# Flamingo gated block on one core: the front reordered (filter, context loads, convolution 0, weights, norms)

## The chip, the cores and the metric

One Trainium2 core runs the whole program. The metric is device time in microseconds (us) of one execution, the median of the runs. The engines are named as in the profile: PE (TensorE matmuls) with PEld (its weight loads), DVE (VectorE), ACT (ScalarE), POOL (GpSimd) and SP (SyncE, here only an issuer of transfers). ACT and POOL issue transfers too. Each engine takes its instructions in order, so an instruction that waits holds up all that stands behind it on its engine.

## The reference, cut to what matters

```python
# x: (16, 256, 256) fp32, ctx: (16, 120, 256) fp32
z  = ctx @ W_in + b_in;  zn = layernorm(z) * g_ln + beta_ln
h  = silu(pe @ Wp1 + bp1) @ Wp2 + bp2            # implicit filter, 512 positions
w  = exp(-arange(512) * exp(a)) [:, None] * h
c  = causal_convolution(zn, w)                   # by FFT in the reference, along the sequence
y  = ffn1(layernorm(x)) * c[:, idx]              # ffn: layernorm, W1a, silu, W1b, + input
x  = x + tanh(g_xattn) * ffn2(y)                 # W2a, silu, W2b
# then a mixture of 16 experts, top 2 of each 32-wide head slice
t  = (layernorm(x) @ Wm + bm).reshape(-1, 32);   gates = top2(softmax(t @ expert_emb))
x  = x + tanh(g_ffn) * (combine(gates, gelu(t @ W1 + b1) @ W2 + b2) @ Wo + bo)
```

## The kernel before, in words

The 4,096 tokens are eight blocks of 512 (4 tiles of 128 tokens). Fp32 weights and activations are split in a high and a low part, and a product is three matmuls of those.

**The front** is ordered by the framework's scheduler from the program's order (up to L953, where `manual_schedule` begins); from there on the order is that of the code. First come the loads: SP's queue takes `cv`, the filter's inputs (`pe`, `Wp1`, `Wp2`), blocks 0 and 1 of x and the first MLP's weights (`w1a`, `w1b`); ACT's queue takes `W_in`, the context in four parts (`load_ctx`, tiles printed as `Y`, in whose storage they lie), `b_in`, `gz` and the rows `bc`. The filter: window exponential (L709), `pe @ Wp1` (L712), silu (L715), `@ Wp2` (L719), times the window (L724) to DRAM as `filt_d`, from which 16 Hankel tiles `hk` are loaded, three buffers deep. The context: eight groups of matmuls (L752 bias, L760), squares for the variance on ACT (L767), gain on DVE (L771); `context_root` (L778 and the steps of `rsqrt_some`, L146 to L165) gives `rz`. `context_norm` writes 32 slices of `zn`: for the first `by_pool` of them ACT scales (L788) and POOL adds the shift (L789), for the others DVE does both (L793).

**The first MLP** (`Mlp1`, blocks 0 to 7) has the steps norm (`normed`: with `off` on ACT, L184; without on DVE, L188), `turn` (transposes L235, copies L237 on ACT and L238 on DVE), `first` (matmuls L205, silu L259 and L260 on ACT, low part L268) and `second` (L293, L278), whose `done` adds the residual (L875) and multiplies by the convolution's result (L876, POOL).

**The convolution** has 16 steps: `conv_mm` (64 matmuls L899, copies `cvs` L906 on ACT, then the next `hk` load) and `conv_turn` (transposes L917, DVE). `mixed` interleaves it: for every second step of the first MLP it takes one step of `side` (the convolution), and for every step one of `weights` (`early_roots`, `early_weights`, which casts `w2` and `v2`). `Mlp2` (0 and 1), `Route(0)` and the first expert stacks are then ordered by hand: `mlp20` is `Mlp2(0)`, `mlp21` is `Mlp2(1)`. `behind_it` places `routes[1]`, `mlps[2]`, the lay-outs (`lay`, which send a normed block through DRAM) and `late_weights`, whose steps load and cast `wm`, `bd`, `wst` (L1035, L1036), and `Wo`.

**The main phase** starts at the first expert step, `hps` (L1257): 256 steps of matmul, gelu on ACT (L1262), second matmul (L1272), gate times output on DVE (L1280) and sum on POOL (L1282); the remaining blocks' MLPs and routes are spread among them.

Of the kernel before, what the change touches and what calls it, by code (L numbers as in the profile page):

```python
# [24 lines left out]
FP = mybir.dt.float32  # L25
FR = mybir.dt.float32r
I32 = mybir.dt.int32
AF = mybir.ActivationFunctionType
ALU = mybir.AluOpType
# [4 lines left out]
P = 128  # L34
# [11 lines left out]
NB = 8  # L46
# [18 lines left out]
XB = 5  # L65
# [28 lines left out]
def block_kernel(  # L94
# [3 lines left out]
    nc = tc.nc  # L98
    dram = ctx.enter_context(tc.tile_pool(name="dram", bufs=1, space=DRAM))
    base = ctx.enter_context(tc.tile_pool(name="base", bufs=1))  # L100
    const = ctx.enter_context(tc.tile_pool(name="const", bufs=1))
# [8 lines left out]
    Y = const.tile([P, NT, D], FP, name="Y")  # L110
    mv1 = const.tile([P, NT, 2], FP, name="mv1")
    mv2 = const.tile([P, NT, 2], FP, name="mv2")
    mv3 = const.tile([P, NT, 2], FP, name="mv3")
# [4 lines left out]
    def scalar(name, func):  # L118
        t = const.tile([P, 1], FP, name=f"s_{name}")
        nc.scalar.activation(t, col(name), func)  # L120
        return t
# [51 lines left out]
    def offset(mean, r, n):  # L173
        off = small.tile([P, n], FP, name="off", tag=f"off{n}", bufs=4 if n == 4 else 2)
        nc.vector.scalar_tensor_tensor(off, mean, -1.0, r, ALU.mult, ALU.mult)
        return off

    def normed(dst, src, mv, t0, r, off=None):

        mean = mv[:, t0 : t0 + 4, 0]  # L180
        for j in range(4):
            c = slice(j, j + 1)
            if off is not None:
                nc.scalar.activation(  # L184
                    dst[:, j, :], src[:, j, :], AF.Identity, bias=off[:, c], scale=r[:, c]
                )
            else:
                nc.vector.tensor_scalar(  # L188
                    dst[:, j, :], src[:, j, :], mean[:, c], r[:, c], ALU.subtract, ALU.mult
                )  # L190
# [126 lines left out]
    class Mlp2:  # L317
# [22 lines left out]
        def prep(self, pool=base, name="n"):  # L340
            t0 = 4 * self.i
            self.n = pool.tile([P, 4, D], FP, name=name, tag=name)
            normed(self.n, Y[:, t0 : t0 + 4, :], mv2, t0, self.r)

        def stream(self):
            t0 = 4 * self.i
# [42 lines left out]
    class Route:  # L389
# [9 lines left out]
        def prep(self):  # L399
            t0 = 4 * self.i  # L400
            y = Y[:, t0 : t0 + 4, :]
            self.n = base.tile([P, 4, D], FP, name="n", tag="n")
            normed(self.n, y, mv3, t0, self.r)

        def shift(self):
            y = Y[:, 4 * self.i : 4 * self.i + 4, :]
# [86 lines left out]
    def some(gen, n=1):  # L493
        for _ in range(n):
            next(gen, None)
# [42 lines left out]
    with ExitStack() as ph:  # L538
# [22 lines left out]
        xs, hankel = {}, {}  # L561

        bc = front.tile([P, NROW], FP, name="bc", bufs=1)
# [37 lines left out]
        window = f1[:, 3 * LF : 4 * LF]  # L601
# [10 lines left out]
        ctx_r = ctx_t.rearrange("(c p) n -> p c n", p=P)  # L612
# [5 lines left out]
        ]  # L618
        z_sb = free[:, NT * D // 2 :].rearrange("p (t j d) -> p t j d", j=4, d=P)

        def load_ctx(g):
            nc.scalar.dma_start(ctx_sb[g], ctx_r[:, :, bass.ts(g, 4 * P)])

        load_ctx(0)
        b_in = front.tile([P, D], FP, name="b_in")
# [10 lines left out]
            )  # L636
        load_x(0)
        for g in (1, 2, 3):
            load_ctx(g)
        w1a = staged(W1a.rearrange("(c p) n -> p c n", p=P), 2, DFF, nc.sync)  # L640
        nc.scalar.dma_start(bc, rows.partition_broadcast(P))
        w1b = staged(W1b.rearrange("(c p) n -> p c n", p=P), NM, D, nc.sync)
        load_x(1)

# [56 lines left out]
        nc.gpsimd.memset(filt, 0.0)  # L701


        ea = scalar("a", AF.Exp)
        tgx = scalar("g_xattn", AF.Tanh)
        tgf = scalar("g_ffn", AF.Tanh)
        nea = const.tile([P, 1], FP, name="nea")
        nc.vector.tensor_scalar(nea, ea, -1.0, None, ALU.mult)
        nc.scalar.activation(window, window, AF.Exp, scale=nea)  # L709
        for m, n in enumerate((P, P, DPOS)):  # L710
            ps = bank("second")
            nc.tensor.matmul(  # L712
# [65 lines left out]
            nc.tensor.matmul(out=var, lhsT=both, rhs=ss, start=True, stop=True)  # L778
            return rsqrt_eps("rz", var, 32, pool=front)

        def context_norm(rz, by_pool=12):
            for n in range(32):
                b, k = n // 2, n % 2
                dst = zn[:, :, k, b : b + 2 * B + 1 : 2 * B]
                z, c = z_sb[:, n // 4, n % 4], rz[:, n : n + 1]
                shift = gz[:, 1].rearrange("p (r e) -> p r e", e=2)
                if n < by_pool:
                    nc.scalar.activation(z, z, AF.Copy, scale=c)  # L788
                    nc.gpsimd.tensor_tensor(  # L789
                        dst, z.rearrange("p (r e) -> p r e", e=2), shift, ALU.add  # L790
                    )
                else:
                    nc.vector.scalar_tensor_tensor(  # L793
                        dst, z.rearrange("p (r e) -> p r e", e=2), c, shift, ALU.mult, ALU.add
                    )
# [19 lines left out]
        def early_roots(first, last):  # L815

            for i in range(first, last):
                if i == NB - 1:
                    while i not in xs:
                        yield  # L820
                    for _ in range(6):
                        yield
                for j in range(4):
                    stats(mv1, 4 * i + j, xs[i][:, j, :])
                    if j % 2:
                        yield
            yield from some_roots(first, last)
            yield
# [122 lines left out]
        rz = context_root()  # L951
# [12 lines left out]
            pass  # L964
        for _ in turn(m0, bank):
            pass
        context_norm(rz)
        for _ in m0.first(bank):
            pass
        for i in range(2, XB):  # L970
            load_x(i)
        t_w2 = staged(W2a.rearrange("(c p) n -> p c n", p=P), 2, DFF, nc.gpsimd)
# [72 lines left out]
        def mixed(gen, n=9):  # L1045
            nonlocal since
            for _ in range(n):
                if next(gen, gen) is gen:
                    break
                since += 1  # L1050
                if since % 2 == 0:
                    some(side)
                some(weights)

        def mlps1(first, last):

# [31 lines left out]
                    pass  # L1088

        mlp20, mlp21, route0 = Mlp2(0), Mlp2(1), Route(0)  # L1090
        mlps1(0, N1)
        cst.close()
        late2 = ctx.enter_context(tc.tile_pool(name="late2", bufs=1))
# [22 lines left out]
        weights = late_weights()  # L1116
# [26 lines left out]
        rest = jobs[5].second(bank)  # L1143
# [14 lines left out]
        def lay(job):  # L1158

            job.lay = early.tile([P, 4, D], FP, name="n1", tag="n1")  # L1160
            for j in (0, 2):
                lay_some(job, j)
            lay_down(job)

        def behind_it():

            yield from ahead
            yield from turn(jobs[7], bank)
            jobs[7].prep_x()
            yield from mlp21.second(bank)  # L1170
            yield from jobs[6].first(bank)
            free.append(place)
            a, m = routes[1], mlps[2]
            some(weights)
            a.norms()
            a.prep()
            rest, soon = jobs[6].second(bank), jobs[7].first(bank)
            for gen in (rest, soon, rest, soon, rest):
                yield next(gen)
            some(weights)  # L1180
            lay(a)
            yield
            yield from rest
            m.prep()
            for _ in soon:
                some(stats_3)
                yield
            lay(m)
            fetch(m)
            nc.scalar.activation(gelu, cv[:, 0:1], AF.Gelu)  # L1190
            some(weights)
            for _ in jobs[7].second(bank):
                some(stats_3)
                yield
# [10 lines left out]
        free, rest = [], behind_it()  # L1205
# [407 lines left out]
```

## Time and profile before

| | before |
|---|---|
| median of 3 runs | 950.46 us (950.06, 950.46, 953.84) |
| the profiled execution | 953.92 us, of which the span is 952.2 us |
| mean granted TensorE clock | 0.981 |
| busy: PE, DVE, ACT, POOL | 904.5, 712.2, 669.9, 566.9 us |
| PE busy in 0 to 253 us / share of that | 225.0 us / 89% |
| DMA share 0 to 10, 10 to 20, 65 to 100 us | 0.84, 0.98, 1.01 |
| first expert step (`hps`) | 253.0 us |

How to read what follows: the page's slices give for 40 equal stretches of the span (23.8 us each) the busy tenths of each engine and the granted PE clock. The chain that ended last is followed back from the last instruction; printed in order of time, each piece has a start, a length, and the engine and line, or the transfer, that it went through. The list of waits adds up the idle time before instructions by the operation that released them ("issue" where nothing that the profile shows was waited for). A timeline prints an engine's instructions in order, with the idle time before them in brackets. DMA shares are of the core's 16 engines, and a stretch can read slightly over 1.

### The profile page before, as it was taken

What the parts mean: (1) busy time and instruction counts of PE and PEld (TensorE: products, weight loads), DVE (VectorE), ACT (ScalarE), POOL (GpSimd) and SP (SyncE); (2) the same over time, 40 slices, a digit from 0 to 9 for tenths busy, and PEclk for the clock granted to TensorE, in tenths of its full rate; (3) what the DMA queues carried; (4) which work ended last, traced back from release to release, by engine and by line L of the source; (5) the groups of instructions that cost most, each with busy time, mean ns of one, the idle gap of its engine ahead of it and who ended that gap; (6) DMA issues with size and microseconds to landing.
All of it is one profiled execution on the core that took longest, in us unless ns stands there. A gap on an engine that the chain in (4) does not pass through costs nothing.

```text
span 952.2 us, 16681 instructions
## 1 busy us (share of the span) xinstructions
PE 904.5 (95%) x6068; PEld 491.2 (52%) x6068; DVE 712.2 (75%) x1297; ACT 669.9 (70%) x856; POOL 566.9 (60%) x459
## 2 busy tenths in 40 slices
PE   5989889899899999999999999999999999989997
PEld 3666667787644545454444454454545444433433
DVE  5585346778977997898799879978985985693343
ACT  4554244667477778878877877788788777778883
POOL 2051113544457768676787777786767866576553
PEclk9889999998999999999999999999999999999998
DMA  7659993232456747846684686478475838646441
GB/s 239 138 151 213 212 187 64 79 107 67 139 133 160 178 128 188 232 113 186 179 199 144 163 219 172 133 188 231 117 189 163 197 112 209 172 129 173 123 124 45
DMA packets 87781, 149.86 MB, mean 157 GB/s; under 512 B 9290, under 2 KB 50762, under 8 KB 87694
## 3 DMA queue, kind: packets, MB, share of 16 engines
q1 hardware_dynamic: 84468, 141.07, 58.4%
q0 software_dynamic: 1296, 4.72, 1.7%
q10 hardware_dynamic: 1936, 3.02, 1.0%
q8 instruction: 47, 0.77, 0.4%
q14 instruction: 34, 0.28, 0.1%
HBM read 120.32 MB, written 28.46 MB: 156 GB/s over the span
## 4 chain that ended last, share of the span: by engine, by line
PE 57%; DVE 21%; issue 7%; DMA 7%; ACT 3%; POOL 3%; SPq 1%; POOLq 0%; DVEq 0%; ACTq 0%
PE hps L1257 19%; PE eo L1272 17%; DVE part L1280 5%; PE aux L1316 4%; DMA gates<-g_d 3%; PE b_conv L899 2%; PE b_second L278 2%; PE b_first L205 2%; PE aux L205 2%; PE aux L1385 1%; DMA hk<-filt_d 1%; DVE bn L170 1%; DMA xb<-in_x 1%; PE aux L1347 1%; DVE n L1407 1%
## 5 line engine op out<-in xcount | busy, mean ns | idle before, releaser
L1262 ACT ACTIVATE hid<-hps 128x1024 f32<-128x1024 f32 x512 | 512.1, 1025 | 144.3 <-PE hps L1257 131.2
L1282 POOL TENSOR_TENSOR comb<-comb,part 128x512 f32<-128x512 f32 x240 | 329.5, 1373 | 159.7 <-DVE part L1280 154.1
L1257 PE MATMUL hps<-stack,wst 98*128 98x512 f32 x1024 | 341.7, 425 | 2.8 <-ACT hid L1262 2.8
L1257 PEld LDWEIGHTS hps<-stack,wst 98*128 98x128 f32 x1024 | 162.6, 189 | 248.5 <-ACT hid L1262 118.6
L1272 PE MATMUL eo<-hid,w2s 128*32 128x512 f32 x2048 | 274.7, 608 | 8.9 <-DVE part L1280 7.1
L1280 DVE SCALAR_TENSOR_TENSOR part<-eo,cv,gates 128x512 f32<-128x512 f32 x237 | 175.4, 743 | 91.2 <-PE eo L1272 71.1
L1272 PEld LDWEIGHTS eo<-hid,w2s 128*32 128x32 f32 x2048 | 40.6, 108 | 103.8 <-issue 49.4
L268 POOL TENSOR_TENSOR s_lo<-silu,s_hi 128x512 fp32r<-128x512 f32 x18 | 23.1, 1291 | 76.1 <-ACT silu L260 61.9
L1375 POOL TENSOR_TENSOR s_lo<-silu,s_hi 128x512 fp32r<-128x512 f32 x24 | 31.0, 1292 | 33.6 <-DVE s_hi L1374 25.5
L1373 DVE SCALAR_TENSOR_TENSOR silu<-silu,u 128x512 f32<-128x512 f32 x24 | 25.7, 1069 | 22.7 <-ACT u L1370 22.7
L259 ACT ACTIVATE s_hi<-b_first,b1f 128x512 fp32r<-128x512 f32 x32 | 21.9, 684 | 28.7 <-PE b_first L205 28.2
L1407 DVE TENSOR_SCALAR n<-Y,mv,r_r 128x256 f32<-128x256 f32 x44 | 37.2, 886 | 3.0 <-POOL nt_lo L1431 3.0
L278 PE MATMUL b_second<-v_hi,s_hi 128*128 128x256 f32 x144 | 38.5, 299 | 0.0
L278 PE MATMUL b_second<-v_lo,s_hi 128*128 128x256 f32 x144 | 36.9, 288 | 0.0
L899 PE MATMUL b_conv<-hk,zn 60*32 60x256 f32 x1024 | 33.0, 379 | 3.2 <-issue 1.7
L1431 POOL TENSOR_TENSOR nt_lo<-n,nt_hi 128x512 fp32r<-128x512 f32 x26 | 33.6, 1294 | 3.1 <-DVE nt_hi L1430 3.1
L906 ACT COPY cvs<-b_conv 128x256 f32<-128x256 f32 x32 | 10.5, 375 | 30.7 <-PE b_conv L899 30.7
L205 PE MATMUL b_first<-nt_hi,w_hi 128*128 128x512 f32 x64 | 28.3, 442 | 2.4 <-ACT silu L260 2.2
L278 PEld LDWEIGHTS b_second<-v_hi,s_hi 128*128 128x128 f32 x144 | 28.4, 198 | 3.4 <-issue 2.9
L278 PEld LDWEIGHTS b_second<-v_lo,s_hi 128*128 128x128 f32 x144 | 28.5, 198 | 0.4
L1430 DVE CAST nt_hi<-n 128x512 fp32r<-128x512 f32 x26 | 28.5, 1096 | 0.0
L1455 POOL TENSOR_TENSOR Y<-Y,tbo 128x256 f32<-128x256 f32 x28 | 28.0, 1012 | 0.0
(282 smaller groups left out, 1488.9 us busy)
## 6 DMA issues: line engine op xcount, KB each, us to landing
gates<-g_d SPq DMA_DIRECT2D x126, 512.0 KB
hk<-filt_d SPq DMA_DIRECT2D x64, 268.1 KB
stack<-t_d SPq DMA_DIRECT2D x48, 256.0 KB
g_d<-gt SPq DMA_DIRECT2D x32, 256.0 KB
n<-laid_d SPq DMA_DIRECT2D x13, 512.0 KB
laid_d<-laid SPq DMA_DIRECT2D x44, 128.0 KB
xr<-in_x SPq DMA_DIRECT2D x8, 512.0 KB
t_d<-t_hi SPq DMA_DIRECT2D x16, 256.0 KB
```

What stands on the lines that cost most here:

```text
L205: nc.tensor.matmul(out=out, lhsT=l, rhs=r, start=(i == 0 and j == 0), stop=(i == n - 1 and j == 2),)
L278: nc.tensor.matmul(out=ps[:, j, :], lhsT=s[k][l][:, c], rhs=v[r][:, k], start=(k == 0 and i == 0 and not (whole and (j or bias))), stop=(k ...
L899: nc.tensor.matmul(out=ps[bass.ts(c, 2 * B), 0:L], lhsT=zn[rows, 4 * n + c, k, e * B : (e + 2) * B], rhs=hk[rows, 2 * c + e, k * SQ : k * ...
L1257: nc.tensor.matmul(out=ps[:, g, :], lhsT=wst[0:KST, e, :], rhs=st[0:KST, 2 * g2 + g, :], start=True, stop=True,)
L1262: nc.scalar.activation(t, ps, AF.Gelu)
L1272: nc.tensor.matmul(out=eo[bass.ts(g, HD)], lhsT=w2s[:, e, :], rhs=hid[g // 2][:, g % 2, :], start=True, stop=True,)
L1280: nc.vector.scalar_tensor_tensor(to, eo, col("b2", e), gs, ALU.add, ALU.mult)
L1282: nc.gpsimd.tensor_tensor(comb, comb, to, ALU.add)
L1316: nc.tensor.matmul(out=ps, lhsT=w[l][:, k, c], rhs=r[:, k], start=(k == 0 and j == 0), stop=(k == 1 and j == 2),)
L1375: nc.gpsimd.tensor_tensor(lo, f, hi.bitcast(FP), ALU.subtract)
L1407: nc.vector.tensor_scalar(job.n[:, j + k, :], Y[:, t0 + k, :], mv[:, t0 + k, 0:1], job.r[:, j + k : j + k + 1], ALU.subtract, ALU.mult,)
L1431: nc.gpsimd.tensor_tensor(lo, src, hi.bitcast(FP), ALU.subtract)
```

## The change

- In the program the filter's exponential stands ahead of the two tanh scalars, and its factor `nea` is made on ACT instead of DVE; in the order that results on ACT it runs ahead of all three silus.
- Context parts 1 to 3 and the rows `bc` are loaded by POOL's queue, part 0 by ACT's as before.
- `context_norm` takes 8 instead of 12 slices by ACT and POOL, does the DVE ones first in program order, and is a generator whose two groups of four are interleaved with `m0.first`.
- One step of the convolution (`some(side)`) stands ahead of the first MLP's second layers.
- In the first 24 steps of `mixed`, `weights` gets two steps at every other turn; `early_roots` waits until its block's load has been issued for every block and six steps more for the last group.
- `Mlp2.prep`, and `Route.prep` for all blocks but block 0, norm with `off`, that is on ACT.
- In `behind_it` the step of `late_weights` that casts `wst` stands behind `lay(a)` instead of ahead of `a.norms()`, and the next one (`Wo`) behind `soon`, ahead of `lay(m)`.

```diff
--- before.py
+++ after.py
@@ -340,7 +340,8 @@
         def prep(self, pool=base, name="n"):
             t0 = 4 * self.i
             self.n = pool.tile([P, 4, D], FP, name=name, tag=name)
-            normed(self.n, Y[:, t0 : t0 + 4, :], mv2, t0, self.r)
+            off = offset(mv2[:, t0 : t0 + 4, 0], self.r, 4)
+            normed(self.n, Y[:, t0 : t0 + 4, :], mv2, t0, self.r, off)
 
         def stream(self):
             t0 = 4 * self.i
@@ -400,7 +401,8 @@
             t0 = 4 * self.i
             y = Y[:, t0 : t0 + 4, :]
             self.n = base.tile([P, 4, D], FP, name="n", tag="n")
-            normed(self.n, y, mv3, t0, self.r)
+            off = offset(mv3[:, t0 : t0 + 4, 0], self.r, 4) if self.i else None
+            normed(self.n, y, mv3, t0, self.r, off)
 
         def shift(self):
             y = Y[:, 4 * self.i : 4 * self.i + 4, :]
@@ -618,8 +620,8 @@
         ]
         z_sb = free[:, NT * D // 2 :].rearrange("p (t j d) -> p t j d", j=4, d=P)
 
-        def load_ctx(g):
-            nc.scalar.dma_start(ctx_sb[g], ctx_r[:, :, bass.ts(g, 4 * P)])
+        def load_ctx(g, queue=nc.scalar):
+            queue.dma_start(ctx_sb[g], ctx_r[:, :, bass.ts(g, 4 * P)])
 
         load_ctx(0)
         b_in = front.tile([P, D], FP, name="b_in")
@@ -636,9 +638,9 @@
             )
         load_x(0)
         for g in (1, 2, 3):
-            load_ctx(g)
+            load_ctx(g, nc.gpsimd)
         w1a = staged(W1a.rearrange("(c p) n -> p c n", p=P), 2, DFF, nc.sync)
-        nc.scalar.dma_start(bc, rows.partition_broadcast(P))
+        nc.gpsimd.dma_start(bc, rows.partition_broadcast(P))
         w1b = staged(W1b.rearrange("(c p) n -> p c n", p=P), NM, D, nc.sync)
         load_x(1)
 
@@ -701,12 +703,13 @@
         nc.gpsimd.memset(filt, 0.0)
 
 
+
         ea = scalar("a", AF.Exp)
+        nea = const.tile([P, 1], FP, name="nea")
+        nc.scalar.mul(nea, ea, -1.0)
+        nc.scalar.activation(window, window, AF.Exp, scale=nea)
         tgx = scalar("g_xattn", AF.Tanh)
         tgf = scalar("g_ffn", AF.Tanh)
-        nea = const.tile([P, 1], FP, name="nea")
-        nc.vector.tensor_scalar(nea, ea, -1.0, None, ALU.mult)
-        nc.scalar.activation(window, window, AF.Exp, scale=nea)
         for m, n in enumerate((P, P, DPOS)):
             ps = bank("second")
             nc.tensor.matmul(
@@ -778,8 +781,9 @@
             nc.tensor.matmul(out=var, lhsT=both, rhs=ss, start=True, stop=True)
             return rsqrt_eps("rz", var, 32, pool=front)
 
-        def context_norm(rz, by_pool=12):
-            for n in range(32):
+        def context_norm(rz, by_pool=8):
+
+            for n in (*range(by_pool, 32), *range(by_pool)):
                 b, k = n // 2, n % 2
                 dst = zn[:, :, k, b : b + 2 * B + 1 : 2 * B]
                 z, c = z_sb[:, n // 4, n % 4], rz[:, n : n + 1]
@@ -789,6 +793,8 @@
                     nc.gpsimd.tensor_tensor(
                         dst, z.rearrange("p (r e) -> p r e", e=2), shift, ALU.add
                     )
+                    if n % 4 == 3:
+                        yield
                 else:
                     nc.vector.scalar_tensor_tensor(
                         dst, z.rearrange("p (r e) -> p r e", e=2), c, shift, ALU.mult, ALU.add
@@ -815,11 +821,11 @@
         def early_roots(first, last):
 
             for i in range(first, last):
-                if i == NB - 1:
-                    while i not in xs:
-                        yield
-                    for _ in range(6):
-                        yield
+                waits = 6 if i >= XB else 0
+                while i not in xs:
+                    yield
+                for _ in range(waits):
+                    yield
                 for j in range(4):
                     stats(mv1, 4 * i + j, xs[i][:, j, :])
                     if j % 2:
@@ -964,9 +970,10 @@
             pass
         for _ in turn(m0, bank):
             pass
-        context_norm(rz)
+        rest = context_norm(rz)
+        some(rest)
         for _ in m0.first(bank):
-            pass
+            some(rest)
         for i in range(2, XB):
             load_x(i)
         t_w2 = staged(W2a.rearrange("(c p) n -> p c n", p=P), 2, DFF, nc.gpsimd)
@@ -1050,7 +1057,8 @@
                 since += 1
                 if since % 2 == 0:
                     some(side)
-                some(weights)
+
+                some(weights, 1 + (since % 2 if since < 24 else 0))
 
         def mlps1(first, last):
 
@@ -1088,6 +1096,7 @@
                     pass
 
         mlp20, mlp21, route0 = Mlp2(0), Mlp2(1), Route(0)
+        some(side)
         mlps1(0, N1)
         cst.close()
         late2 = ctx.enter_context(tc.tile_pool(name="late2", bufs=1))
@@ -1171,20 +1180,20 @@
             yield from jobs[6].first(bank)
             free.append(place)
             a, m = routes[1], mlps[2]
-            some(weights)
             a.norms()
             a.prep()
             rest, soon = jobs[6].second(bank), jobs[7].first(bank)
             for gen in (rest, soon, rest, soon, rest):
                 yield next(gen)
+            lay(a)
             some(weights)
-            lay(a)
             yield
             yield from rest
             m.prep()
             for _ in soon:
                 some(stats_3)
                 yield
+            some(weights)
             lay(m)
             fetch(m)
             nc.scalar.activation(gelu, cv[:, 0:1], AF.Gelu)
```

## The prediction

> **What bounds the kernel now.** I read the page's slices first. The second half of the span is TensorE-bound (PE digits of 9) and the diff leaves its order alone, so whatever is won or lost must come before the first expert step, which the chain places at 253.04 us (`hps`, L1257). In front of it PE is less full and its clock, the third row, falls to 8 twice.
>
> ```profile
> PE   5989889899899999999999999999999999989997
> PEclk9889999998999999999999999999999999999998
> DMA  7659993232456747846684686478475838646441
> ```
>
> Next the chain that ended last, in order of time (start us, us, what), without the window. It gives the front its price list.
>
> ```profile
> 6.39 9.28 DMA xb<-in_x
> ...
> 20.64 2.08 ACT xb L184 x4
> 22.72 0.94 ACT v_hi L958
> 23.66 0.02 issue
> 23.68 1.28 ACT L715
> 24.97 0.69 ACT hk L715
> 25.66 0.04 issue
> 25.71 3.78 PE b_conv L719 x4
> ...
> 51.52 3.63 ACT Y L788 x12
> ...
> 56.34 4.61 PE b_first L205 x12
> ```
>
> The third silu of the filter stands in ScalarE's queue behind block 0's norm (which waits for x) and a cast. PE then waits 3.27 us for it and runs four matmuls at 0.945 us each; the eight before took 3.70 us, 0.46 each. At 51.52 twelve ScalarE copies of the context norm stand ahead of the first MLP's silu.
>
> Then PE's waits between 60 and 165 us (line, waited for, total us, times, longest):
>
> ```profile
> PE b_second L278 <- issue: 2.0, 1, 2.0
> PE b_turn L235 <- DVE nt_lo L238: 2.0, 1, 2.0
> PE b_conv L899 <- issue: 1.7, 1, 1.7
> PE b_conv L899 <- ACT cvs L906: 1.3, 1, 1.3
> ```
>
> These are most of 8.4 us of PE idle there. Last, ScalarE's timeline around 170 us (start, duration, then the idle time before it), since the change puts new work there:
>
> ```profile
> 168.63 2.08 ACT L184 ACTIVATE n<-xb,off,r_r 128x256 f32<-128x256 f32 x4 [0.77 <-DVE off L175]
> 170.62 2.06 ACT L184 ACTIVATE xb<-xb,off,r_r 128x256 f32<-128x256 f32 x4
> ...
> 175.69 1.07 ACT L237 CAST stack<-b_conv 128x512 fp32r<-128x512 f32 x2 [2.19 <-PE b_conv L235]
> ```
>
> About 4.75 us, 0.5%, is what a measurement of this kernel can tell from no change. The sum is made against the profiled execution, 953.92 us (span 952.2); the median of the runs, 950.46, is 3.46 lower.
>
> **Part 1: exponential first, nea on ScalarE.** The window's exponential moves ahead of all three silus, and x's norm behind them. Two of four table loads (1.28 us each) go, and so does the 3.27 us wait. If Wp1 lands as now (8.07 us), the filter's and the context's matmuls follow each other: PE ends the first layer near 12.9, the second plus the first context group near 20.5, and seven groups of 2.33 us end near 36.8 instead of 46.07. The squares and the gain products then limit: the chain of ScalarE and VectorE still holds block 1's norm, so the root's matmul (L778, now 47.78) comes at 39.2 to 42.7. Two bounds: 8.5 us earlier, or, if x and `bc` land late (part 2), 2.5. I take 6, nearer to the first since the wait and the cold matmuls (3.3 + 1.9) are certain to be removed from PE's path.
>
> **Part 2: context 1 to 3 and `bc` on GpSimd's queue.** ScalarE's first instruction now waits to 10.03 behind its own issues; four of them leave. On GpSimd an issue takes 0.75 to 0.84 us (L574, in this trace), so 3.1 us stand ahead of all its set-up, which ends near 10 instead of 6.5; the identity and `bz` (8.48) come later, and the first context group with them, but not before PE has the filter's first layer to do. `bc` is fourth on that queue, and VectorE's use of it (L667, L668) stands ahead of x's statistics; behind that wait are VectorE's norm chain (15.70 to 20.3) and ScalarE's norm. From the x load's issue at 6.39 to landing at 15.67 I estimate 12 to 19 us for `bc`. Cost nothing to 4 us, inside part 1's bounds.
>
> The bytes stay and only the order of landing changes: DMA share is 0.84 in 0 to 10 us and 0.98 in 10 to 20. A rule of the Trainium skill speaks against this edit: "DMA: Bandwidth & Descriptors", section "Issuing engines are not separate DMA queues", says that transfers of all issuers run on the same 16 engines, and that a second issuer saves only the sequencer's time. The row agrees that the engines are full; by the rule alone part 2 would be worth at most the issue time and part 1 would keep its lower half.
>
> **Part 3: the context norm.** ScalarE's copies fall from 12 to 8, four ahead of the first silu (1.2 us by 3.63/12) and four behind it; VectorE takes 24 rows of 0.498 us (20 took 9.96): 12.0 us. Writing r for what part 1 brings, the rows are ready at 63.5 − r instead of 61.48, while PE's first layer, without its 2.16 us wait and most of its slow matmuls, ends near 58.0 − r instead of 60.95 − r.
>
> **Part 4: convolution 0 ahead of the second layer.** It needs all 32 rows, so the PE time from 58.0 to 63.6 (5.6 us) stands idle where now L278 and L235 (2.75 us) lie, and the convolution then runs cold, 3.5 instead of 1.96. The point reached at 65.5 now comes at 69.7 − r: cost 4.2. Back comes that each later convolution is one slot ahead: the 1.73 and 0.2 us behind the filter's load `hk`, at 85.7 and 78.9, are covered, if DMA (share 1.01 from 65 to 100 us) keeps pace.
>
> **Part 5: second weights sooner.** At 120 to 131 us the cast of v2 (1.04) splits two silus, its GpSimd part (2.34) stretches VectorE, and PE waits 1.29 + 0.25 + 1.99 us and runs slow for 1.2. Spread earlier, most of it goes. With part 4's waits, the idle and slow time before 173.6 falls from 10.2 to an estimated 4 (2.5 to 9: at the upper end the same casts only hit other silus). Parts 4 and 5: +4.2 − 6.2 = −2.0.
>
> **Part 6: norms on ScalarE.** For Mlp2(0) the four scalings leave VectorE (1.38 us at 173.90) for ScalarE, where the order puts them ahead of the two norms that now run at 168.63 in idle time. But their operands are ready only at 174.1 (VectorE's root ends at 173.86). Queued behind the waiting instruction: eight scalings (4.14 us), two casts (0.60 + 0.40), then the stack copies of L237. These move from 175.69 to 174.1 + 2.08 + 4.0 + 0.9 ≈ 181.1, less 1 us of overlap at most, and PE's L205 from 178.34 to 182.5. PE has nothing to put there: +4.2. Behind two gaps near 229, 2.05 us in all, matmuls take 0.63 instead of 0.40 until 237; a gap of 5.5 us should cost 1 to 2 more. I take +5.5, range 3.5 to 7.5. For the clock, "TensorE: Matmul & The Clock Gate", Part 1 (the HAM clock gate), has half clock after about 3.4 us idle and full clock after as much work: an estimate of 1.7 us for this gap, none for the 2 us gap, where the trace shows a loss. Mlp2(1)'s norm finds ScalarE idle (4.7 us at 190) and costs nothing; without that cover, 2.1. Route(1)'s and Mlp2(2)'s take 1.39 and 2.9 us off VectorE, where the loads of their laid-out copies wait for them either way.
>
> **Part 7: `wst` copies behind the lay-out.** Two GpSimd subtractions of 2.4 us at 234.9 now stretch VectorE's root (L157 2.23, L158 2.35). Moved, the last waits fall by 0 to 2, I take 1. They must end before `hps` at 253; at about 248 they have some 3 us of cover, else PE waits for the difference. Wo's load, moved past SP's four lay-outs, is used 30 steps later.
>
> **Sum.** −6 (1, 2) −2 (3 to 5) +5.5 (6) −1 (7) = −3.5: 950.4 for the profiled execution, 947.0 against the median. Best ends: −8.5 −3.5 +3.5 −2 = −10.5; worst: −2.5 +3 +7.5 +0 = +8.
>
> **The rivals.**
> *Front's full gain.* x and `bc` land in time (r = 8.5), the idle and slow time falls to 3 (−3), and ScalarE's queue costs its plain 4.2: −7.3 − 1 = −8.3, about 942. For: DMA has landed most bytes by 20 us in any order. Against: VectorE's chain is unshortened. 0.33 together with anything better.
> *ScalarE's queue at 174 us decides.* The norm heading that queue costs its upper price, 7.5, and the lead held when it is reached is only 1: r at 2.5, and parts 3 to 5 at +1.5 (idle and slow time cut to 7.5 instead of 4). With part 7 at 0 that is −1 + 7.5 = +6.5: 957. It decides against the change once the price exceeds the lead at 173 us by 4.75. For: the operands' time, 174.1, and the 4.14 us of scalings behind them are plain in the trace. Against: so small a lead needs x late by as much as the whole removed wait. 0.13.
> *The change doesn't do what it says.* Exponential first still leaves PE waiting, since Wp1 and x land later behind the four new GpSimd issues; gains and costs cancel: 950. 0.14, within 0.5%.
>
> **How the numbers follow.** My forecast, −3.5 and its near surroundings, gets 0.40, all of it within 0.5% but for 0.07 that falls beyond −4.75. Faster: 0.33 + 0.07 = 0.40; same: 0.33 + 0.14 = 0.47; slower 0.13. The range goes from 941.0, just past the full front gain, to 954.0, short of the slower rival; some 0.1 is left out on either side.
>
> **What would show it.** In the changed profile: one silu table load before 20 us and no gap before L722; L781 near 42; PE idle some 5 us ahead of the first L905; no two-microsecond waits between 115 and 131; ScalarE's copies of L237 near 181 less the lead, with PE idle about 5 us there; the first `hps` near 249.5 instead of 253. Wrong if the norm's instruction at 174 finds its operands earlier than ScalarE reaches it, or if convolution 0 waits much longer than its rows.

## The result: 0.9% slower, and where the profile after lost it

The changed kernel takes 960.47 us (median of 20 runs, 958.07 to 969.75), the kernel before 952.09 (20 runs beside them). The ratio is 1.0088, 95% interval 1.0067 to 1.0109: 8.4 us slower, where 947 was forecast. The profiled execution spans 958.7 us against 952.2.

PE's work is the same instruction for instruction, so the span can be divided where PE has done the same matmuls. The marks are the first matmul, the end of block 0's first layer (333 matmuls later), the end of block 4's second layer (1,483 more), the first L205 of Mlp2(0), the L293 that PE starts after a wait at 228.67 (239.26 after), and the first `hps`. The forecast is the prediction's sum, laid on these stretches:

| stretch of PE's work | before, us | after, us | difference | forecast |
|---|---|---|---|---|
| to the first matmul | 8.07 | 10.62 | +2.55 | 0 |
| to the end of block 0's first layer | 52.88 | 45.13 | −7.75 | −9 |
| to the end of block 4's second layer | 112.65 | 122.69 | +10.04 | +1 |
| to Mlp2(0)'s first layer | 4.74 | 8.71 | +3.97 | +4.2 |
| to L293 | 50.33 | 52.11 | +1.78 | +1.3 |
| to the first `hps` | 24.21 | 21.58 | −2.63 | −1 |
| sum | 252.88 | 260.84 | +7.96 | −3.5 |

The spans differ by 6.5 us, since behind the first `hps` the changed kernel takes 1.4 us less. The third row is the failure; the first two together come 3.8 us short. The page's slices of the changed kernel:

```profile
PE   5977989799899999999999999999999999989997
PEclk9998999899989999999999999999999999999999
DMA  7759992124445936865694667568656847655442
```

PE is less full than before in its third and fourth slices (48 to 96 us) and in the eighth. DMA still shows its block of nines. The chain that ended last, in order of time (start us, us, what), names the places:

```profile
1.83 8.66 DMA hk<-in_Wp
...
10.62 5.64 PE b_second L715 x6
16.26 3.71 PE b_conv L722 x4
...
56.38 2.95 issue
59.32 3.66 PE b_conv L905 x64
...
81.11 1.86 PE b_conv L905 x52
82.97 1.89 issue
84.86 0.64 PE b_conv L905 x9
...
87.75 0.24 DVE off L175 x2
88.00 0.34 DVE n L188
88.33 0.03 issue
88.36 2.07 ACT xt L184 x4
90.43 0.57 ACT s_hi L259
91.00 0.58 ACT silu L260
91.58 0.04 issue
91.63 2.93 PE b_first L205 x6
...
131.99 1.06 PE b_second L278 x9
133.05 3.52 issue
136.57 0.52 PE b_second L278 x3
```

The filter's weights land at 10.6 instead of 8.1 us, and the first matmuls run slow. Convolution 0 waits for `zn` and takes 3.66 us instead of 1.96. At 91.6 PE waits for a silu behind a norm and a VectorE root. At 83 and at 133 PE stops in the middle of a group, waiting for nothing that the profile shows. PE's list of waits between 60 and 165 us (line, waited for, total us, times, longest) has the same in short; the waits at 120 to 131 that part 5 was to remove are gone, but PE is idle there for 11.0 us instead of 8.4:

```profile
PE b_second L278 <- issue: 3.5, 1, 3.5
PE b_first L205 <- ACT silu L260: 3.4, 1, 3.4
PE b_conv L905 <- issue: 2.5, 2, 1.9
PE b_turn L235 <- DVE nt_lo L238: 1.0, 1, 1.0
PE b_first L205 <- DVE nt_lo L238: 0.7, 1, 0.7
```

ScalarE's timeline at Mlp2(0) (start, duration, and the idle time before) is as forecast: 6.2 us of waiting ahead of the norm, two norms of block 5 behind it, and only then L237:

```profile
179.01 2.07 ACT L184 ACTIVATE n<-Y,off,r_r 128x256 f32<-128x256 f32 x4 [6.23 <-DVE off L175]
180.99 2.06 ACT L184 ACTIVATE n<-xb,off,r_r 128x256 f32<-128x256 f32 x4
182.95 2.06 ACT L184 ACTIVATE xb<-xb,off,r_r 128x256 f32<-128x256 f32 x4
...
185.74 1.05 ACT L237 CAST stack<-b_conv 128x512 fp32r<-128x512 f32 x2
```

### The profile page after: what moved, and what is told of

Its sections match the earlier page's. It is cut to its first block, busy times and chain, and to the rows that moved or that the text cites. A ratio compares the mean times of both kernels' runs of the same rounds, so it can differ in the third digit from the quotient of the medians.

```text
span 958.7 us, 16680 instructions
## 1 busy us (share of the span) xinstructions
PE 905.2 (94%) x6068; PEld 488.6 (51%) x6068; DVE 704.8 (74%) x1286; ACT 674.7 (70%) x867; POOL 568.7 (59%) x459
## 4 chain that ended last, share of the span: by engine, by line
PE 61%; DVE 19%; issue 8%; DMA 5%; POOL 3%; ACT 3%; SPq 1%; POOLq 0%; DVEq 0%; ACTq 0%
PE hps L1266 19%; PE eo L1281 17%; DVE part L1289 5%; PE aux L1325 5%; PE b_conv L905 4%; PE b_first L205 3%; PE b_second L278 3%; DMA gates<-g_d 2%; PE aux L205 2%; DMA t_d<-t_lo 2%; PE b_conv L205 1%; PE b_turn L923 1%; DMA hk<-in_Wp 1%; DVE ex L371 1%; PE b_conv L722 1%
## 5 line engine op out<-in xcount | busy, mean ns | idle before, releaser
L1291 POOL TENSOR_TENSOR comb<-comb,part 128x512 f32<-128x512 f32 x240 | 329.4, 1372 | 159.3 <-DVE part L1289 153.6
L905 PE MATMUL b_conv<-hk,zn 60*32 60x256 f32 x1024 | 36.9, 414 | 6.0 <-issue 6.0
L1382 DVE SCALAR_TENSOR_TENSOR silu<-silu,u 128x512 f32<-128x512 f32 x24 | 25.1, 1044 | 23.1 <-ACT u L1379 23.0
L278 PE MATMUL b_second<-v_hi,s_hi 128*128 128x256 f32 x144 | 36.4, 287 | 0.0
L205 PE MATMUL b_first<-nt_hi,w_hi 128*128 128x512 f32 x64 | 27.5, 430 | 5.4 <-ACT silu L260 5.1
L905 PEld LDWEIGHTS b_conv<-hk,zn 60*32 60x32 f32 x1024 | 21.0, 114 | 17.1 <-issue 10.6
```

Of the source, the lines that this page charges most:

```text
L205: nc.tensor.matmul(out=out, lhsT=l, rhs=r, start=(i == 0 and j == 0), stop=(i == n - 1 and j == 2),)
L278: nc.tensor.matmul(out=ps[:, j, :], lhsT=s[k][l][:, c], rhs=v[r][:, k], start=(k == 0 and i == 0 and not (whole and (j or bias))), stop=(k ...
L905: nc.tensor.matmul(out=ps[bass.ts(c, 2 * B), 0:L], lhsT=zn[rows, 4 * n + c, k, e * B : (e + 2) * B], rhs=hk[rows, 2 * c + e, k * SQ : k * ...
L1291: nc.gpsimd.tensor_tensor(comb, comb, to, ALU.add)
```

## The experiments

Two theories of the third stretch stood against each other. Theory A: the order of the queues, above all convolution 0 ahead and the weights' pace. Theory B: the loads; the DMA engines are full from 60 to 150 us in both kernels (share 0.96 and 0.98), and what PE saves in one place it waits for in the next. Each ratio is against runs of the kernel before on the same chip beside it; 0.001 is 0.95 us. A difference between two ratios is uncertain by 0.003 to 0.005.

**One part undone in the changed kernel** (1.0088, and 1.0107 when it was run again).

`u_conv0`, without the step ahead:

```diff
-        some(side)
         mlps1(0, N1)
```

> The changed kernel without the one step of the convolution ahead of the first MLP's second layers (part 4 undone alone). Theory A, the order: of the 10.0 us that PE loses between the end of block 0's first layer and the end of block 4's second layer, the wait for all rows of zn (3.6 us) and the slow first convolution (3.66 against 1.96 us) go, and so does the 3.4 us wait for ScalarE's silu at 91.6, since the transposes and the root steps that stood behind convolution 4 in VectorE's queue move back: 5 to 8 us faster than the changed kernel, about 953 to 956. Theory B, the loads: PE waits there for its own instructions and for the filter tiles, because the DMA engines are full (share 1.0), and a wait removed in one place comes back in the next: 0 to 2 us faster.

Measured: 1.0015 (0.9988 to 1.0042), 7 us below the changed kernel. That is theory A's number, but not for its reason: the wait for the silu is still there (3.88 us, at 82.9).

`u_mlp20`, Mlp2(0)'s norm on VectorE:

```diff
-            off = offset(mv2[:, t0 : t0 + 4, 0], self.r, 4)
+            off = offset(mv2[:, t0 : t0 + 4, 0], self.r, 4) if self.i else None
```

> The changed kernel with Mlp2(0)'s norm back on VectorE (part 6 undone for that block alone). Theory A, ScalarE's queue: PE's wait at 184.4 to 187.2 and the slow matmuls up to 239 go, 4 to 6 us faster than the changed kernel. Rival: the four scalings on VectorE stretch its queue instead (they took 1.38 us there) and the stage behind, where VectorE is 70% busy, gives it back: 1 to 2 us faster.

Measured: 1.0025 (0.9996 to 1.0054), 6 us below. In its trace the stretch to Mlp2(0)'s first layer is 4.78 us again. Theory A.

`u_ctx`, the loads back on ScalarE's queue:

```diff
-            load_ctx(g, nc.gpsimd)
+            load_ctx(g)
-        nc.gpsimd.dma_start(bc, rows.partition_broadcast(P))
+        nc.scalar.dma_start(bc, rows.partition_broadcast(P))
```

> The changed kernel with context parts 1 to 3 and bc back on ScalarE's queue (part 2 undone alone). Theory A: the filter's first weights land at 8.1 instead of 10.5 us and PE starts 2.4 us earlier; ScalarE is held by its issues until 10, but its first work is needed only at 12: 1.5 to 3 us faster than the changed kernel. Rival: the front's end is set by the last context part and by VectorE, so that the earlier start is lost again by the root of the context norm: no change (0 plus or minus 1).

Measured: 1.0071 (1.0035 to 1.0107), not told from the changed kernel. The traced execution is a short one (955.8 us, where the median is 960.9). In it the first matmul does come at 8.14 us, the first layer ends at 52.8 instead of 55.8, and the third stretch takes 121.3, so that the lead is kept; over all runs no gain is seen. What part 2 costs stays open.

`u_pace`:

```diff
-                some(weights, 1 + (since % 2 if since < 24 else 0))
+                some(weights)
```

> The changed kernel with one step of the weights at every step of mixed, as before (part 5 undone, the waits of early_roots kept). Theory A: the doubled pace put root steps and the casts of w2 and v2 ahead of the first MLP's work in VectorE's queue (PE waits at 91.6 and 110), so that undoing it gives 1 to 4 us. Rival, as the prediction had it: the sooner casts keep the 120 to 131 us stretch free, and undoing it costs 3 to 5 us.

Measured: 1.0077 (1.0045 to 1.0110): neither forecast, no difference seen. In its trace the silu's wait goes, and PE waits 1.48 and 2.17 us for `hk` before 75.8 and 78.6 instead, which is theory B's sign.

**The loads left out.** `nohk_before` and `nohk_after` use the first three filter tiles for all sixteen steps and leave out the loads of the other thirteen:

```diff
             if n + NH < NK:
-                load_hankel(n + NH)
+                hankel[n + NH] = hk
```

> The kernel before, with only the first three filter tiles loaded: steps 3 to 15 of the convolution use the three tiles again, so 13.9 MB of loads between 65 and 150 us are left out. Theory B, the loads: TensorE's gaps that fall at a fixed count of its instructions (at matmul 727 and 853 of the trace, and every 126 from there; 4.3 us in the stretch from the end of block 0's first layer to the end of block 4's second) are waits for its own program, fetched through the same DMA engines; with the engines free they go, and the waits for hk with them: the stretch falls from 112.6 to about 107 us, the kernel by 4 to 6. Theory A, the order: the engines' queues set the stretch, and it stays within 1.5 us.

> The changed kernel with the same loads left out (steps 3 to 15 of the convolution use the first three tiles). Theory B: the 9.5 us of gaps at the fixed counts go, with the slow matmuls behind them; the stretch falls from 122.7 to 108 to 111 us, the kernel by 10 to 14, and stands within 3 us of the kernel before with the same loads left out, or below it, apart from the 5.8 us of part 6. Theory A: the loss of the order stays, and the stretch is still 8 to 10 us longer than in the kernel before without these loads.

Measured: 0.9883 (0.9841 to 0.9924) and 0.9954 (0.9927 to 0.9980). Without these loads (DMA share from 60 to 150 us 0.16 and 0.12) the kernels gain 11 and some 13 us, and the changed one is still 7 slower. The third stretch is 104.8 us before and 113.1 after. So both theories hold a part: the loads cost both kernels 8 to 10 us of it, and some 8 of the 10 us between them are order. In `nohk_after` the wait for `zn` (3.55 us) and a silu's wait (3.8 us) are still there. In the waits of `nohk_before` from 60 to 165 us, every "issue" is gone:

```profile
PE b_turn L235 <- DVE nt_lo L238: 2.0, 1, 2.0
PE b_conv L899 <- ACT cvs L906: 1.4, 1, 1.4
PE b_conv L235 <- DVE n L188: 0.8, 1, 0.8
PE b_second L278 <- DVE s_lo L268: 0.4, 1, 0.4
PE b_turn L917 <- DVE Y L927: 0.3, 1, 0.3
```

**One part alone in the kernel before.** `a_front` has parts 1 to 3 of the diff, `f_conv0` those and the step ahead, `a_pace` part 5, `a_mlp20` this:

```diff
-            normed(self.n, Y[:, t0 : t0 + 4, :], mv2, t0, self.r)
+            off = None if self.i else offset(mv2[:, t0 : t0 + 4, 0], self.r, 4)
+            normed(self.n, Y[:, t0 : t0 + 4, :], mv2, t0, self.r, off)
```

> The kernel before with parts 1 to 3 alone (exponential first, context loads on two queues, context norm by 8 and interleaved). By the stages of the changed kernel's trace PE ends block 0's first layer 5.2 us sooner (55.8 against 60.95). Theory A (the order sets the stretch behind it): 3 to 5 us faster than the kernel before. Theory B (the stretch behind is bound by the filter tiles' loads, which take some 85 us from the first convolution on): the first loads start 3 to 4 us sooner at the same pace, 2 to 4 us faster. If the early wait for zn's rows (61.5 less the gain, against VectorE's 24 rows of 0.5 us) eats it: 0.

> The kernel before with parts 1 to 4: as a_front, and one step of the convolution ahead of the first MLP's second layers. Theory A: against a_front PE waits 3.6 us for zn and runs the first convolution at the slow clock, +1.7, less what the later steps get back: 3 to 6 us slower than a_front. Prediction's part 4 with its return: 2 slower. Theory B: within 1 of a_front, since the loads of the filter tiles start at the same time either way.

> The kernel before with part 5 alone (two steps of the weights at every other turn, and early_roots' waits). The waits at 120 to 131 us (1.29 + 0.25 + 1.99, and 1.2 of slow matmuls) go: -3 to -5. Against that the root of blocks 3 and 4 comes ahead of block 2's norm in VectorE's queue, as in the changed kernel, where PE then waited 3.4 us and ran slow for about 2: +4 to +5. Theory A: these cancel, within 2 of the kernel before. As predicted: 4 to 6 faster.

> The kernel before with Mlp2(0)'s norm alone on ScalarE. As predicted and as the changed trace's stages have it (8.7 against 4.75 us, and 1.8 us of slow matmuls behind): 5 to 6 us slower than the kernel before. Rival: half of it is taken up by the waits at 228 and 246 us, which this kernel still has: 2 to 3 slower.

Measured: `a_front` 0.9987 (0.9963 to 1.0010), `f_conv0` 1.0034 (1.0008 to 1.0059), `a_pace` 0.9984 (0.9962 to 1.0007), `a_mlp20` 1.0055 (1.0029 to 1.0082). The front alone is most likely worth 1.2 us, and perhaps nothing; the step ahead costs 4.5 on top of it; the pace is most likely worth 1.5, and perhaps nothing; the norm costs 5.3, where 5.5 was forecast.

**What the step ahead costs.** `few_rows` takes away its wait: it leaves out 12 of the 24 rows of `zn` that VectorE writes (they are set to zero beforehand):

```diff
-            for n in (*range(by_pool, 32), *range(by_pool)):
+            for n in (*range(by_pool, 20), *range(by_pool)):
```

> The changed kernel with 12 of the 24 rows of zn that VectorE writes left out (they stay zero): VectorE is through 6 us sooner, and convolution 0 finds its rows when PE ends the first layer. Theory A (part 4's price is the wait for these rows and the slow clock behind it): the 3.6 us gap goes and the first convolution takes about 2 us instead of 3.7: 4 to 6 faster than the changed kernel. Theory B (the filter tiles' loads set the stretch): the loads start 5 sooner, but PE waits for them later on: 1 to 3 faster.

Measured: 1.0080 (1.0050 to 1.0109), beside 1.0107 (1.0076 to 1.0138) for the changed kernel in the same rounds: 2.6 us, which the intervals don't tell from nothing. Convolution 0 starts without a gap, at 53.5, and PE's waits from 54 to 165 us show where the time went:

```profile
PE b_first L205 <- ACT silu L260: 3.4, 1, 3.4
PE b_turn L235 <- DVE nt_lo L238: 3.0, 2, 2.1
PE b_conv L905 <- issue: 1.8, 2, 1.1
PE b_second L278 <- issue: 1.7, 1, 1.7
PE b_conv L905 <- DMA hk<-filt_d: 1.6, 1, 1.6
```

Put beside each other, the traces show what the step ahead does (us; the start of ScalarE's copy of a convolution's result, and the end of block 4's second layer):

| | convolution 0 | convolution 15 | between | block 4's end | behind convolution 15 |
|---|---|---|---|---|---|
| before | 65.6 | 155.4 | 89.8 | 173.6 | 18.2 |
| a_front | 59.3 | 151.6 | 92.3 | 169.8 | 18.2 |
| f_conv0 | 62.1 | 153.6 | 91.5 | 175.0 | 21.3 |
| changed | 63.0 | 157.2 | 94.2 | 178.4 | 21.3 |
| few_rows | 55.5 | 155.0 | 99.6 | 176.4 | 21.3 |
| nohk_before | 62.8 | 144.8 | 82.0 | 163.0 | 18.2 |
| nohk_after | 61.3 | 146.0 | 84.8 | 167.4 | 21.4 |

With the loads, the sixteen convolutions take 90 to 100 us; without them 82 to 85. An early start is mostly lost on the way: in `few_rows` the first comes 7.5 us sooner than in the changed kernel, the last 2.2. So the loads hold back the convolutions, and PE fills the time between with the first MLP's layers. One step ahead puts one more slot of that MLP work, 3.1 us, behind the last convolution, where it covers no wait for a load. The other part of the price is the wait for `zn` at the start: in `a_front` PE waits 0.9 us there, since the second layer's first part stands ahead.

**Where the norm costs.** `late_n` issues Mlp2(0)'s norm just ahead of its transposes:

```diff
-        mlp20.prep()
         some(weights)
...
+        mlp20.prep()
         whole(turn(mlp20, last_bank, place))
```

> The changed kernel once more, beside the three that follow, so that their differences are taken on the same chip in the same rounds: 6 to 10 us above the kernel before. By the parts measured alone (front -1.2, convolution 0 ahead +4.5, pace -1.5, Mlp2(0)'s norm +5.3, the rest about -2) it should stand 5 above; what is over that is the interplay of pace and convolution 0.

> The changed kernel with Mlp2(0)'s norm still on ScalarE, but issued behind block 5's norm and the casts of wm and bd, just ahead of its transposes. Theory A (the price is the queue: eight scalings wait behind an instruction whose operands are not there): PE's L205 comes at about 183.5 instead of 187.2 of the profiled span, 3 to 5 us faster than the changed kernel. Rival (the price is ScalarE's own time for the norm, 2.1 us, and the longer way through it): within 1 of the changed kernel.

Measured: the changed kernel again, 1.0107; `late_n` 1.0100 (1.0065 to 1.0136). No gain, but no answer either: `prep` also computes the offsets on VectorE, and these moved behind a residual sum that waits for a load, so that the norm began at 185.0. `late_n2` leaves them in their place (`prep` then takes them from `self.off`) and moves the four scalings alone:

```diff
-        mlp20.prep()
+        mlp20.off = offset(mv2[:, 0:4, 0], mlp20.r, 4)
         some(weights)
...
+        mlp20.prep()
         whole(turn(mlp20, last_bank, place))
```

> As late_n, but the offsets of Mlp2(0)'s norm stay where the changed kernel computes them on VectorE (in late_n they had moved behind a residual sum that waits for a load, and came at 185.0 instead of 179.0 less 0.2). Theory A (the price is ScalarE's queue behind the waiting instruction): block 5's norm runs in the idle time before, the norm follows at about 179 to 181, PE's L205 comes 8.7 - 4 = about 5 us behind the end of block 4's second layer instead of 8.7: 3 to 5 us faster than the changed kernel's 962.8. Rival (ScalarE's own time): within 1 of it.

Measured: 1.0030 (1.0007 to 1.0053), 5.5 to 7 us below the changed kernel (1.0088 and 1.0107). In ScalarE's timeline the two norms of block 5 run first, in time that was idle, and L237 follows Mlp2(0)'s norm at once:

```profile
171.76 2.08 ACT L184 ACTIVATE n<-xb,off,r_r 128x256 f32<-128x256 f32 x4 [0.77 <-DVE off L175]
173.75 2.06 ACT L184 ACTIVATE xb<-xb,off,r_r 128x256 f32<-128x256 f32 x4
...
177.22 2.07 ACT L184 ACTIVATE n<-Y,off,r_r 128x256 f32<-128x256 f32 x4 [0.59 <-DVE off L175]
179.86 0.59 ACT L237 CAST stack<-b_conv 128x512 fp32r<-128x512 f32 x1 [0.57 <-PE b_conv L235]
```

The stretch to Mlp2(0)'s first layer is 5.31 us instead of 8.71. The place in the queue was the price, not ScalarE's time.

**Versions that keep the parts worth keeping.** `best2` undoes parts 2, 4 and 6 (for Mlp2(0)); `best1` the pace too; `best3` undoes 4 and 6 only; `best4` is `best3` with the doubled pace later:

```diff
-                some(weights, 1 + (since % 2 if since < 24 else 0))
+                some(weights, 1 + (since % 2 if 6 < since < 30 else 0))
```

> The changed kernel with parts 2 (context loads), 4 (convolution 0 ahead) and 6 for Mlp2(0) undone; the exponential first, the context norm with 8, the pace of the weights, Route's norm on ScalarE and the later wst copies stay. If the undone parts' costs add up (0 to 3, 3 to 8 and 5 to 6 us): 9 to 14 us below the changed kernel, 3 to 5 below the kernel before. If the stretch with the filter tiles is bound by their loads: 6 below the changed kernel, about 2 above the kernel before.

> As best2, with the pace of the weights undone too: what then stays of the change is the exponential first, the context norm with 8 interleaved, Route's and Mlp2(1)'s norms on ScalarE and the later wst copies. Theory A (the doubled pace harms): 2 to 4 us below best2. Rival (it helps): 2 to 4 above.

> The changed kernel without the convolution step ahead and with Mlp2(0)'s norm on VectorE; all else of the change stays, the context loads on two queues too. If the parts measured alone add up (-1.2 - 1.5 - 2): 4 to 6 us below the kernel before, 10 to 14 below the changed one. If pace and front have nothing to add to each other, because both end in the same loads of the filter tiles: 2 below the kernel before.

> As best3, with the doubled pace of the weights only from step 7 to 29, so that the root of blocks 3 and 4 stands behind block 2's norm in VectorE's queue: the 3.75 us wait of PE at 83.8 and the slow clock behind it go. If that wait counts: 3 to 5 us faster than best3 (951.7), 5 to 6 below the kernel before. If the loads of the filter tiles set the stretch: within 1.5 of best3, since PE waits for hk or its program instead.

Measured: `best2` 0.9957 (0.9924 to 0.9990), `best1` 0.9980 (0.9951 to 1.0009), `best3` 0.9982 (0.9959 to 1.0006), `best4` 0.9974 (0.9950 to 0.9997). `best2` and `best4` are faster than the kernel before, by some 2 to 4 us; which is best is not told. In `best4` PE waits for no engine from 60 to 165 us. All of its waits are "issue"; all but one of 0.65 us are of the kind that went when the loads were left out:

```profile
PE b_conv L905 <- issue: 4.8, 4, 2.1
PE b_turn L923 <- issue: 2.1, 2, 1.8
PE b_turn L235 <- issue: 2.1, 1, 2.1
```

## Why the prediction was wrong

**Parts 1 and 2, −6: mis-sized.** Measured alone with part 3, −1.2 (−3.5 to +1). Three things were wrong. First, "if Wp1 lands as now (8.07 us)" was taken as given: in the thirteen traces with the context on two queues PE's first matmul comes at 9.4 to 10.6, in the seven with one queue at 7.7 to 8.1. The rule that the prediction quoted from the Trainium skill ("DMA: Bandwidth & Descriptors", section "Issuing engines are not separate DMA queues") was the better guide to part 2: a second queue only put other bytes ahead of these. (The row of L574 has issues of 0.75 to 0.91 us on GpSimd, not 0.75 to 0.84; the four of the changed kernel take 2.9 us, near the forecast 3.1.) Second, of the 5.2 us that were "certain to be removed" the wait went, but four matmuls of L722 run slow again, at another place (0.93 us each, against 0.46 for the fast ones before). From 10.6 on PE is busy without a gap to 45.7 us, so the root came at 45.7, not at 39.2 to 42.7. Third, the profile of before was an execution in which x landed late. The same front in four traces of the unchanged order has x at 15.7, 15.4, 14.6 and 12.7 us and block 0's first layer ending at 60.95, 60.7, 58.2 and 53.4. The gap that part 1 removes is as long as x is late; with the changed front x lands at 15.9 to 17.0 and the layer ends at 53.3 to 55.8. The forecast priced the latest landing of the four. And a lead at this point is not kept: `a_front`'s trace ends the first layer 7.2 us sooner than the kernel before, and block 4's second layer 3.8.

**Parts 4 and 5, −2: the step that failed** is the refund, −6.2 us of idle and slow time. PE's time in the third stretch of the two traces divides as follows (us; a stop is explained in the last section):

| | before | after |
|---|---|---|
| "issue" stops at a fixed count of matmuls | 4.25 | 5.99 |
| wait for `zn` ahead of convolution 0 | 0 | 3.55 |
| wait for a silu at 91.6 us | 0 | 3.36 |
| other waits | 4.56 | 2.03 |
| PE busy | 103.84 | 107.76 |
| sum | 112.65 | 122.69 |

Convolution 0's own price is the 3.55 and the 1.70 us that it ran slow, 5.25 together; that is less than the 7.1 which the prediction's terms give for the two (5.6 of waiting, 3.5 − 1.96 of slow running). What is left of the +10.04 is +4.8, in the place of the −6.2. The prediction put the 1.73 us at 85.7 "behind the filter's load `hk`", to be covered if DMA keeps pace; its own list of waits has "issue" there, and it was a stop of the other kind, which no reordering here removed. The other waits did shrink, 4.56 to 2.03, and part 5's casts did leave 120 to 131 us. But each step of `weights` also issues VectorE's roots, and these came ahead of block 2's norm: the silu's wait of 3.4 us, with slow matmuls behind it; in `u_pace`'s trace this wait is gone. And the slot of MLP work that came to lie behind the last convolution (21.3 against 18.2 us) was not in the sum. On the front alone the step ahead costs 4.5 us net, within the changed kernel 7: nothing of the refund is to be seen. Undoing the pace in the changed kernel gains nothing, alone the pace is not told from nothing, and `best4`, without the silu's wait, is not told from `best3`: its "issue" stops are longer in turn (8.4 against 6.5 us in the traces).

**Part 6, +5.5: right**, in size (5.3 alone, 5.5 to 7 undone) and in mechanism, by `late_n2`.

**Part 7, −1: right in sign**, −2.6 by the stretch before `hps`; not run alone. That stretch takes 21.6 to 23.1 us in the fourteen traces that have part 7, and 24.2 to 27.0 in the six without; but the fourteen also have Route's norm on ScalarE.

Of the rivals, the one on the slower side came nearest with 957, in part by luck. Its question was the right one, the price at 174 us against the lead held there. But its price, 7.5, was too high, and the lead that it put at 1 was −4.84 us (178.44 against 173.60): the larger part was lost before the norm was reached. The measured +8.4 lies past even the worst end of the sum, +8. What stays open is some 4 us: the parts measured alone (−1.2 + 4.5 − 1.5 + 5.3 − 2.6 = +4.5) don't reach 8.4, and the step ahead costs more within the changed kernel than on the front alone. Both differences are near the intervals, and no run separates pace and step ahead.

## What to carry to other kernels

Where a chain of loads holds back a stretch, look at what lies behind the last load, not only at the waits within the stretch: here a wait removed there mostly came back elsewhere, and work moved behind the last load covered no load any more. A wait that the profile calls "issue" is not one for a load or an engine until something shows it: find out what it is before counting on its going. Moving an operation to an idle engine is priced by its place in that engine's queue: ask when its operands are there, and what that could have run meanwhile stands behind it. A gap seen in one profile is worth what it is on average; look in a second execution for what made it before pricing its removal.

## What the runs showed of the hardware

PE stops for its own program. The page lists 47 packets, 0.77 MB, that is 16 KB each, in the queue "q8 instruction":

```profile
q8 instruction: 47, 0.77, 0.4%
```

PE executes 6,068 matmuls and as many weight loads, some 258 instructions to a packet. Counting from the start (stretch, PE busy, PE count, ...), the "issue" gaps begin here in the kernel before:

```profile
0.00:85.60 85.60, 71.39 (x727) 49.71 (x727) 54.63 (x169) 40.27 (x127) 25.35 (x48) 0.92 0.72 182
0.00:96.20 96.20, 80.26 (x853) 56.24 (x853) 61.17 (x198) 45.35 (x137) 25.35 (x48) 0.93 0.75 186
0.00:113.10 113.10, 95.10 (x1105) 67.64 (x1106) 65.17 (x212) 49.40 (x146) 28.80 (x52) 0.94 0.79 190
```

and here in the changed one:

```profile
0.00:83.00 83.00, 66.61 (x725) 45.20 (x726) 57.28 (x175) 34.96 (x118) 25.04 (x46) 0.98 0.75 187
0.00:124.20 124.20, 101.86 (x1229) 70.67 (x1230) 77.58 (x237) 49.94 (x149) 33.82 (x54) 0.96 0.83 187
0.00:133.10 133.10, 110.19 (x1355) 76.92 (x1356) 81.80 (x249) 54.69 (x159) 33.82 (x54) 0.96 0.84 188
```

727, 853, 1105 and 725, 1229, 1355 (some two records are missing there) lie 126 or a multiple of it apart, whatever instruction stands there. The gaps are 0.3 to 3.5 us long, differ from execution to execution, and go when the filter tiles' loads go. (The gap at 56.4 in the changed kernel is not of this kind: VectorE writes its last rows of `zn` until 59.5, and in `few_rows`, with 12 rows fewer, there is no gap.) In the trace's record of DMA packets the packet of such a gap can be found, here from 84 to 85 us of the kernel before and from 133 to 134 us of the changed one:

```profile
q8 instruction: 1, 0.02, 7.9%
q8 instruction: 1, 0.02, 10.4%
```

The first starts at 84.64 us and lands at 85.90, and PE goes on at 87.44. The second starts at 133.51 and lands at 135.17, and PE goes on at 136.57. The 20 traces of this case have 67 gaps of 0.3 us or more at these counts between 60 and 170 us, and every one ends 1.3 to 1.7 us after its packet has landed; at the other crossings the packet landed at least 1.0 us ahead. In the 18 traces with the loads these gaps add up to 2.3 to 8.4 us, whatever the order of the kernel; in the two without there is none. So PE waits there for its program. That the packets come late because the other transfers fill the engines fits the two runs without the loads; by what way is not seen.

The Trainium skill, "Runtime: NRT & Kernel Launch", section "Instruction fetch mechanics", has a program streamed in blocks of 16 KiB, 256 instructions, at a cost that is mostly hidden. The block's size agrees; hidden it is not here, where the DMA share from 60 to 150 us is 0.96 before and 0.98 after.

A gap of 3.5 us also cost PE its clock. Convolution 0, behind the wait for `zn`, took 3.66 us against 1.96 before: the granted clock is 0.54 from 59.3 to 63.0 us and 1.00 from 65.6 to 67.6. The convolution behind the gap at 133 us took 2.95. In `few_rows`, without that wait, convolution 0 took 1.96.
